# A deformable-convolution network: the first pair's sums moved to the front, its weights spread by three engines, and half of its rows kept on chip

## The chip, the cores and the metric

The kernel runs on one core of a Trainium2 chip. The metric is the device time of the whole program in microseconds (us). Five engines work side by side, each in the order of its own list of instructions: TensorE (PE: matrix products and transposes), VectorE (DVE), ScalarE (ACT), GpSimd (POOL) and SyncE (SP), which here does nothing but issue transfers. ACT and POOL issue transfers too. An engine waits at an instruction until the semaphores that it names are reached, and everything behind it in that engine's list waits with it.

## The reference, cut to what matters

The input `x` has 8 images of 64 channels and 128 x 128 pixels. Four layers follow one another, each `x = x + layer(groupnorm(x))`: a deformable convolution (layer 0), a 3x3 convolution, a two-way state-space scan, and a layer of nearest neighbours. Only layer 0 is touched, and of it only the beginning:

```
xn     = groupnorm(x)                        # 32 groups: two channels each, over all pixels
offset = conv(xn, wh: 1x15) + conv(xn, wv: 15x1) + bh + bv      # 18 maps
mask   = sigmoid(conv(xn, wm: 3x3) + bm)                         # 9 maps
y      = sum over 9 taps of wd[tap] @ (mask * bilinear sample of xn at pixel + tap + offset)
x      = x + relu(batchnorm(y))
```

The group's mean and variance need all pixels of an image before one of them can be normalized; the samples of a pixel can lie anywhere in the image.

## The kernel before, in words

Two images of 64 channels fill the 128 partitions, so the work goes by 4 pairs. For each pair layer 0 has these parts, all in `deform` (lines 177 to 446, with its helpers):

- `statistics(p)` (L262): eight loads of 16 rows (128 x 2048, 1 MB each) into two alternating buffers `xs`; VectorE takes the sums of 512 columns at a time (`bn_stats`, L269); `groupnorm` (L139) makes from them the scale `r` and the bias `nb` (L147).
- `fill(p)` (L274): the same eight pieces are loaded again (L287, tile `xt`, the same two buffers), ScalarE normalizes each in place (L288), PE transposes four rows at a time (L291, 33 steps `g`), VectorE and ScalarE copy the transposed rows out of PSUM into `q` (L293 to L295; three buffers), and SP writes `q` to two tables in DRAM (L301), in which an entry holds a pixel and the one below it with all 64 channels. With the rim of zeros around it, one entry and its neighbour give all four corners of a bilinear sample in 1 KB.
- `offsets(p, e)` (L305): for 8 rows at a time, a piece `xe` of `x` is loaded (L311) and normalized (L312), PE makes the three convolutions at once with block-diagonal weights `wt` (L323, tile `po`, one PSUM buffer), ScalarE adds the bias (`ob`, L333), PE transposes the maps (`to`, L336), and `positions` (L342) turns them into indices and weights on VectorE (L350 to L372).
- `sample(p, g, ...)` (L377): GpSimd issues 9 indirect loads for each of 8 blocks of a row group (L389, tile `g`, four buffers of 9 loads); VectorE multiplies and adds the corners (L398, L399), PE transposes (L403), ScalarE copies (L406), PE applies `wd` (L412).

Before the first `sample`, the kernel has to make: zero rims of four tables (L198 to L206, from a tile `zeros`), the loads and the spreading of the weights into `wt` (L207 to L223: from the loaded `whv` and `wmm`, 28 copies on VectorE, 28 on GpSimd, 2 sums and 18 more copies on VectorE), the bias, `statistics(0)`, `fill(0)` and `offsets(0, 0)`. Then the loop at the end of `deform` (from L427 on) runs `sample` for pair 0, with small steps of the next `offsets` and of `far` mixed in: `far` is the setup of layers 2 and 3 (`self.setup`, many small loads and small VectorE operations), then `statistics` and `fill` of the next pair. After all pairs, `rest` does the other layers.

The order written in Python isn't the order on the chip: a scheduler of the framework orders each engine's list by dependencies and by its own estimate of times, gives buffers out, and lets an instruction whose inputs are ready move up. So the setup of layers 2 and 3 begins in the very first microseconds. Two of its habits matter here. A buffer that is allocated where an earlier one was released waits for the readers of the earlier one: in the kernel before, the buffers `xs` lie over the setup tiles `zeros`, `whv` and `wmm`. And all transfers of SP and ACT share eight completion semaphores in turn, so that a transfer is not issued before the one eight places ahead of it in the common order has landed.

Of the kernel before, what the change touches and what calls it, by code (L numbers as in the profile page):

```python
# [9 lines left out]
F32 = mybir.dt.float32  # L10
# [6 lines left out]
P = 128  # L17
C = 64
H = 128
HW = H * H  # L20
CH = 512
NCH = HW // CH
ROOM = 2 * (H // 2 + 1) * H
CELL = H + 3
LINE = H + 4
PW = 2 * C
# [15 lines left out]
class Net:  # L42
# [134 lines left out]
    def deform(self):  # L177
        tc, nc, ins = self.tc, self.nc, self.ins
# [4 lines left out]
        at = {t: n for n, t in enumerate(taps)}  # L183
        with ExitStack() as ctx:
# [4 lines left out]
            wt = cp.tile([P, len(taps), 3, 2, 9], F32, name="wt")  # L189
            nc.gpsimd.memset(wt, 0.0)  # L190
            bias = cp.tile([54, 1], F32, name="bias")
# [1 line left out]


            tables = [[self.dram.tile([CELL, LINE, PW], F32, name=f"table{s}{i}") for i in range(2)] for s in range(min(2, self.npair))]
            with tc.tile_pool(name="a_setup", bufs=1) as sp:
                zeros = sp.tile([P, 2 * PW], F32, name="zeros")
                nc.gpsimd.memset(zeros, 0.0)  # L198
                for table in (t for pair in tables for t in pair):
                    flat = table.rearrange("a b q -> a (b q)")  # L200
                    n = LINE * PW // P
                    for row in (0, CELL - 1):
                        nc.scalar.dma_start(flat[row : row + 1, :].rearrange("a (p n) -> (a p) n", p=P), zeros[:, 0:n])
                    for r0, r1 in ((1, CELL - 1 - 1), (CELL - 2, CELL - 1)):
                        nc.scalar.dma_start(flat[r0:r1, 0 : 2 * PW], zeros[0 : r1 - r0, :])
                        nc.scalar.dma_start(flat[r0:r1, (LINE - 2) * PW :], zeros[0 : r1 - r0, :])  # L206
                whv = sp.tile([P, 2, 15, 2, 9], F32, name="whv")  # L207
                wmm = sp.tile([P, 9, 9], F32, name="wmm")
                for i in range(2):
                    rows = slice(i * C, (i + 1) * C)  # L210
                    nc.sync.dma_start(whv[rows, 0], ins["wh"])
                    nc.sync.dma_start(whv[rows, 1], ins["wv"])
                    nc.sync.dma_start(wmm[rows], ins["wm"])
                for i in range(2):
                    rows = slice(i * C, (i + 1) * C)
                    for d in range(-7, 8):
                        if d:
                            nc.vector.tensor_copy(wt[rows, at[0, d], 0:2, i, :], whv[rows, 0, d + 7])
                            nc.gpsimd.tensor_copy(wt[rows, at[d, 0], 0:2, i, :], whv[rows, 1, d + 7])
                    nc.vector.tensor_add(wt[rows, 0, 0:2, i, :], whv[rows, 0, 7], whv[rows, 1, 7])  # L220
                    for a in range(3):
                        for b in range(3):
                            nc.vector.tensor_copy(wt[rows, at[a - 1, b - 1], 2, i, :], wmm[rows, 3 * a + b])  # L223
                bh = sp.tile([36, 2], F32, name="bh")
                for d in range(2):
                    for i in range(2):
                        to = slice(18 * d + 9 * i, 18 * d + 9 * i + 9)
                        for n, b in enumerate(("bh", "bv")):
                            nc.sync.dma_start(bh[to, n : n + 1], ins[b][d].rearrange("(k o) -> k o", o=1))
                nc.vector.tensor_add(bias[0:36, :], bh[:, 0:1], bh[:, 1:2])  # L230
                for i in range(2):
                    nc.sync.dma_start(bias[36 + 9 * i : 45 + 9 * i, :], ins["bm"].rearrange("(k o) -> k o", o=1))
            wt = wt.rearrange("p t d i k -> p t (d i k)")
            wd = cp.tile([P, 5, C], F32, name="wd")
            nc.sync.dma_start(wd[:, 0:4, :], ins["wd"][0:512].rearrange("(j p) o -> p j o", p=P))
            nc.sync.dma_start(wd[0:C, 4, :], ins["wd"][512:576])

            xp = pool("a_x", 2)
            ep = pool("a_e", 2)
# [19 lines left out]
            norms = {}  # L259
            ready = {}  # L260

            def statistics(p):  # L262

                st = wp.tile([P, NCH, 6], F32, tag="gst", name=f"st{p}")
                for n in range(8):
                    xs = xp.tile([P, 2048], F32, tag="xs", name=f"xs{p}_{n}")
                    nc.sync.dma_start(xs, self.x[p * P : (p + 1) * P, n * 2048 : (n + 1) * 2048])
                    for m in range(4):
                        nc.vector.bn_stats(st[:, 4 * n + m, :], xs[:, m * CH : (m + 1) * CH])  # L269
                    yield  # L270
                norms[p] = self.groupnorm(wp, ps_s1, "s1", st, "gn0")
                yield

            def fill(p):  # L274

                r, nb = norms[p]
                table = tables[p % len(tables)]

                q = qp.tile([P, 2, 4, 2, C], F32, tag="q", name=f"q{p}_0")
                nc.gpsimd.memset(q[:, :, 0, 0, :], 0.0)  # L280
                for g in range(NCH + 1):
                    n = 4 if g < NCH else 1
                    if g < NCH:
                        if g % 4 == 0:
                            xs = xp.tile([P, 16, H], F32, tag="xs", name=f"xt{p}_{g}")
                            xf = xs.rearrange("p h w -> p (h w)")
                            nc.sync.dma_start(xf, self.x[p * P : (p + 1) * P, g * CH : (g + 4) * CH])  # L287
                            nc.scalar.activation(xf, xf, AF.Identity, bias=nb, scale=r)  # L288
                        tp = ps_t.tile([P, 4, 2, C], F32, tag="tp", name=f"tp{p}_{g}")
                        for m in range(4):  # L290
                            nc.tensor.transpose(tp[:, m].rearrange("p i c -> p (i c)"), xs[:, 4 * (g % 4) + m, :], self.ident)  # L291
                        nxt = qp.tile([P, 2, 4, 2, C], F32, tag="q", name=f"q{p}_{g + 1}")
                        nc.vector.tensor_copy(q[:, :, :, 1, :].rearrange("p i r c -> p r i c"), tp)  # L293
                        nc.scalar.copy(q[:, :, 1:4, 0, :].rearrange("p i r c -> p r i c"), tp[:, 0:3])
                        nc.vector.tensor_copy(nxt[:, :, 0, 0, :], tp[:, 3])  # L295
                    else:
                        nc.gpsimd.memset(q[:, :, 0, 1, :], 0.0)
                    for i in range(2):
                        rows = table[i][4 * g + 1 : 4 * g + 1 + n]
                        src = q[:, i, 0:n].rearrange("p r t c -> p r (t c)")  # L300
                        nc.sync.dma_start(rows[:, 2 : 2 + H, :].rearrange("r w e -> w r e"), src)  # L301
                    q = nxt
                    yield
# [114 lines left out]
            def run(steps):  # L418
                for _ in steps:
                    pass  # L420

            run(statistics(0))
            run(fill(0))
            run(offsets(0, 0))
            for p in range(self.npair):  # L427
                more = p + 1 < self.npair
                far = chain(statistics(p + 1), fill(p + 1)) if more else iter(())
                if p == 0:  # L430
                    far = chain(self.setup(ps_s1, "s1"), far)
                for e in range(NCH // 2):
                    if e == NCH // 2 - 1:
                        run(far)
                    nxt = (p, e + 1) if e + 1 < NCH // 2 else (p + 1, 0)
                    near = offsets(*nxt) if nxt[0] < self.npair else iter(())
                    count = [0]

                    def work(near=near, far=far, count=count):
                        count[0] += 1  # L440
                        next(near, None)
                        if count[0] % 3 == 0:
                            next(far, None)

                    idx, wts = ready.pop((p, e))
                    for half in range(2):
                        sample(p, 2 * e + half, tables[p % len(tables)], idx, wts[half], work)
                    run(near)
# [930 lines left out]
```

## Time and profile before

| what | us |
|---|---|
| median of 3 runs | 16689.37 |
| lowest and highest | 16679.99 and 16696.37 |
| the profiled execution, its own time | 16687.07 |
| its span | 16685.0 |
| PE / VectorE / ScalarE / GpSimd busy in the span | 11226.6 / 11600.4 / 2990.4 / 10394.8 |
| first and last start of a gather (L389) | 167.9 and 11883.7 |

The profile is of one execution; times in it count from the start of its span, which is 2.07 us shorter than that execution's time. A line of a timeline has start, duration, engine, source line, operation, output and input, and in brackets how long the engine had been idle and what ended that. "SPq" and "ACTq" are issues of transfers. A "window" table has the busy time of each engine in a stretch, the granted clock of PE as a share of full speed, and how busy the 16 DMA engines were.

### The profile page before, as it was taken

How to read it: one execution, taken by the hardware profiler on the slowest of the kernel's cores; microseconds unless marked ns; L12 is line 12 of the kernel's file. 1: busy time of each engine (PE TensorE's matmuls, PEld its weight loads, DVE VectorE, ACT ScalarE, POOL GpSimd, SP SyncE). 2: the span in 40 equal slices, each digit the busy share in tenths (PEclk: the TensorE clock that was granted, in tenths of full speed). 3: DMA queues.
4: the chain of work that ended last, by engine and by line, in shares of the span. 5: the costliest groups of instructions: out<-in, count | busy, mean ns of one | idle time of the engine just before them, and what ended most of it. 6: DMA issues, size and time to landing. Idle time of an engine off the chain costs nothing. (4 is left out here: it accounts for less than half of the span.)

```text
span 16685.0 us, 119663 instructions
## 1 busy us (share of the span) xinstructions
PE 11226.6 (67%) x31864; PEld 4101.4 (25%) x31864; DVE 11600.4 (70%) x27208; ACT 2990.4 (18%) x5596; POOL 10394.8 (62%) x10484
## 2 busy tenths in 40 slices
PE   6766565756576655667566566663489888988896
PEld 1211111111111111111111111111144344444443
DVE  6777777777777777777777777777557557566566
ACT  1101111111110011111000110100144243243342
POOL 4777777777777777777777777777434134043142
PEclk9987787878787787878778788776689899999897
DMA  5334444444433344443333333333322433424223
GB/s 172 120 115 128 133 130 135 136 131 134 137 120 112 114 129 130 135 131 120 112 114 113 118 115 114 118 110 108 118 67 68 148 77 104 112 78 133 85 67 103
DMA packets 900631, 1937.61 MB, mean 116 GB/s; under 512 B 199916, under 2 KB 435828, under 8 KB 876404
## 3 DMA queue, kind: packets, MB, share of 16 engines
q0 software_dynamic: 442368, 1208.55, 24.4%
q1 hardware_dynamic: 383204, 684.00, 13.4%
q10 hardware_dynamic: 74384, 37.40, 1.1%
q8 instruction: 260, 4.26, 0.1%
q14 instruction: 415, 3.40, 0.1%
HBM read 1544.92 MB, written 208.10 MB: 105 GB/s over the span
## 5 line engine op out<-in xcount | busy, mean ns | idle before, releaser
L389 POOL DMA_INDIRECT g<-table,idx x9216 | 8908.4, 967 | 2809.5 <-issue 2613.6
L398 DVE TENSOR_TENSOR g<-g,wts 128x256 f32<-128x256 f32 x9216 | 3818.1, 420 | 3101.9 <-DMA g<-table,idx 3084.0
L399 DVE TENSOR_REDUCE sm<-g 128x64 f32<-128x256 f32 x9216 | 4988.3, 580 | 0.8 <-DVE pos L353 0.2
L323 PE MATMUL po<-xe,wt 128*54 128x512 f32 (+3 forms) x8384 | 4734.9, 676 | 44.4 <-ACT ob L333 42.5
L403 PE MATMUL sp<-ident,sm 128*128 128x128 f32 x4096 | 1525.1, 377 | 4117.6 <-DVE sm L399 4100.3
L403 PEld LDWEIGHTS sp<-ident,sm 128*128 128x128 f32 x4096 | 626.2, 155 | 6897.7 <-DVE sm L399 4964.4
L406 ACT COPY s<-sp 128x512 f32<-128x512 f32 x1024 | 600.0, 586 | 8514.1 <-PE sp L403 8514.1
L323 PEld LDWEIGHTS po<-xe,wt 128*54 128x54 f32 x8384 | 929.9, 140 | 1417.2 <-issue 1069.3
L840 POOL COPY l_yb<-ln_y 128x512 f32<-128x512 f32 x128 | 79.1, 659 | 1303.9 <-PE l1v L834 1161.4
L412 PE MATMUL yp<-s,wd 128*64 128x512 f32 (+1 forms) x2560 | 808.1, 652 | 12.6 <-ACT s L406 12.6
L1206 POOL TENSOR_TENSOR u<-u,v 128x512 f32<-128x512 f32 x256 | 330.7, 1292 | 697.4 <-DVE v L1205 519.7
L563 PE MATMUL c<-room,l_w 128*64 128x508 f32 (+1 forms) x3072 | 741.3, 597 | 21.1 <-DMA room<-nx 14.9
L1298 POOL TENSOR_TENSOR ms<-ms,ln_y 128x512 f32<-128x512 f32 x256 | 278.4, 1107 | 738.8 <-DVE ln_y L119 706.7
L1188 ACT ACTIVATE fx<-room,ln_b,ln_g 128x512 f32<-128x512 f32 x512 | 639.2, 1293 | 116.2 <-DMA in<-fx 97.9
L405 PE MATMUL s<-ident,sm 128*64 128x128 f32 x1024 | 345.9, 338 | 363.1 <-DVE sm L399 336.1
L1221 DVE TENSOR_TENSOR_SCAN z<-tabs,z,u 128x256 f32<-128x256 f32 x512 | 444.9, 902 | 208.3 <-POOL u L1206 192.9
L1199 PE MATMUL pv<-in,tabs 128*128 128x512 f32 x1024 | 537.2, 649 | 46.2 <-DVE u L1205 46.2
L1268 PE MATMUL py<-x,outs 128*128 128x512 f32 x1024 | 506.0, 599 | 4.6 <-POOL x L1253 4.2
L1268 PE MATMUL py<-in,outs 128*128 128x512 f32 x1024 | 505.7, 606 | 1.6 <-ACT h L1270 1.2
L1285 PE MATMUL pc<-outs,h 128*128 128x256 f32 x2048 | 498.9, 394 | 9.9 <-DVE h L1271 8.8
L1253 POOL TENSOR_TENSOR x<-x,xt 128x512 f32<-128x512 f32 x256 | 350.6, 1370 | 126.3 <-DVE xt L1252 126.0
L1285 PEld LDWEIGHTS pc<-outs,h 128*128 128x128 f32 x2048 | 382.5, 195 | 168.7 <-issue 65.4
(406 smaller groups left out, 10008.7 us busy)
## 6 DMA issues: line engine op xcount, KB each, us to landing
g<-table,idx POOLq DMA_INDIRECT x9216, 2.7
in<-fx SPq DMA_DIRECT2D x1024, 128.0 KB
xe<-in_x_dram SPq DMA_DIRECT2D x56, 1408.0 KB
table<-q SPq DMA_DIRECT2D x256, 256.0 KB
xs<-in_x_dram SPq DMA_DIRECT2D x32, 1024.0 KB
xt<-in_x_dram SPq DMA_DIRECT2D x32, 1024.0 KB
y<-ys SPq DMA_DIRECT2D x128, 256.0 KB
room<-in_x_dram SPq DMA_DIRECT2D x64, 512.0 KB
```

The lines of the kernel that those rows point to most:

```text
L323: nc.tensor.matmul(po[:, r0:r1, c0:c1], lhsT=wt[:, t, :], rhs=xe[:, row + r0 : row + r1, c0 + dx : c1 + dx], start=n == 0, stop=n == len(u ...
L389: nc.gpsimd.indirect_dma_start(out=tq[:, k, :], out_offset=None, in_=flat[i], in_offset=bass.IndirectOffsetOnAxis(ap=idx[:, at : at + 1], ...
L398: nc.vector.tensor_mul(t[:, k], t[:, k], w)
L399: nc.vector.tensor_reduce(sm[:, k], t[:, k].rearrange("p q c -> p c q"), axis=mybir.AxisListType.X, op=ALU.add)
L403: nc.tensor.transpose(sp[:, j, :], sm[:, j * P : (j + 1) * P], self.ident)
L406: nc.scalar.copy(st[i][:, 0:4, m * P : (m + 1) * P], sp)
L412: nc.tensor.matmul(yp[i * C : (i + 1) * C, :], lhsT=wd[0:rows, j, :], rhs=st[i][0:rows, j, :], start=j == 0, stop=j == 4)
L563: nc.tensor.matmul(o, lhsT=lt, rhs=mv, start=k < 2, stop=k >= len(calls) - 2)
L1188: nc.scalar.activation(fx[:, e].rearrange("p h (o m) -> p h o m", m=self.INNER), src[:, e::2], AF.Identity, bias=w["ln1_b"], scale=w["ln1_g"])
L1199: nc.tensor.matmul(pv, lhsT=tabs[:, at : at + P], rhs=fx[:, :, h, :], start=h == 0, stop=h == 1)
L1268: nc.tensor.matmul(py, lhsT=lt, rhs=mv, start=n == 0, stop=n == len(calls) - 1)
L1285: nc.tensor.matmul(pc[:, i], lhsT=hs[:, h, i, m * P : (m + 1) * P], rhs=self.outs[:, CEN : MIX + P], start=True, stop=True)
```

## The change

The setup block before the pools is gone; what it did stands now behind `statistics(0)`. Three edits:

1. `statistics(0)` comes first, and its pieces are loaded before anything else on SP. The loads of `wh`, `wv`, `wm` and the biases are issued by ACT instead of SP. The zero rims follow behind the weights on ACT. Since the setup tiles are now allocated after the buffers `xs`, these no longer lie over them.
2. Of the copies that spread the weights, the 28 of `wh` go from VectorE to ScalarE (`nc.scalar.copy`); GpSimd keeps its 28 and VectorE its 20 others.
3. Pieces 4 to 7 of the first pair's eight are loaded into four buffers of their own (`kept`, 32 KB on each partition), which hold them from the sums to the tables; `fill(0, kept)` loads pieces 0 to 3 again and takes 4 to 7 from there. The pool closes after `fill(0)`. Other pairs pass no `kept` and run as before.

```diff
-            with tc.tile_pool(name="a_setup", bufs=1) as sp:
-                zeros = sp.tile([P, 2 * PW], F32, name="zeros")
-                nc.gpsimd.memset(zeros, 0.0)
-                ... (zero rims, loads and copies of the weights, biases: as below, loads on nc.sync)
-                            nc.vector.tensor_copy(wt[rows, at[0, d], 0:2, i, :], whv[rows, 0, d + 7])
-                            nc.gpsimd.tensor_copy(wt[rows, at[d, 0], 0:2, i, :], whv[rows, 1, d + 7])
             wd = cp.tile([P, 5, C], F32, name="wd")
-            nc.sync.dma_start(wd[:, 0:4, :], ins["wd"][0:512].rearrange("(j p) o -> p j o", p=P))
-            nc.sync.dma_start(wd[0:C, 4, :], ins["wd"][512:576])
...
-            def statistics(p):
+            def statistics(p, kept=()):
...
-                    xs = xp.tile([P, 2048], F32, tag="xs", name=f"xs{p}_{n}")
+                    xs = kept[n] if n in kept else xp.tile([P, 2048], F32, tag="xs", name=f"xs{p}_{n}")
...
-            def fill(p):
+            def fill(p, kept=()):
...
-                            xs = xp.tile([P, 16, H], F32, tag="xs", name=f"xt{p}_{g}")
-                            xf = xs.rearrange("p h w -> p (h w)")
-                            nc.sync.dma_start(xf, self.x[p * P : (p + 1) * P, g * CH : (g + 4) * CH])
+                            held = g // 4 in kept
+                            xf = kept[g // 4] if held else xp.tile([P, 2048], F32, tag="xs", name=f"xt{p}_{g}")
+                            xs = xf.rearrange("p (h w) -> p h w", w=H)
+                            if not held:
+                                nc.sync.dma_start(xf, self.x[p * P : (p + 1) * P, g * CH : (g + 4) * CH])
                             nc.scalar.activation(xf, xf, AF.Identity, bias=nb, scale=r)
...
-            run(statistics(0))
-            run(fill(0))
+            with tc.tile_pool(name="a_first", bufs=1) as fp:
+                kept = {n: fp.tile([P, 2048], F32, name=f"kept{n}") for n in range(4, 8)}
+                run(statistics(0, kept))
+                with tc.tile_pool(name="a_setup", bufs=1) as sp:
+                    ...
+                        nc.scalar.dma_start(whv[rows, 0], ins["wh"])
+                        nc.scalar.dma_start(whv[rows, 1], ins["wv"])
+                        nc.scalar.dma_start(wmm[rows], ins["wm"])
+                    ...
+                                nc.scalar.copy(wt[rows, at[0, d], 0:2, i, :], whv[rows, 0, d + 7])
+                                nc.gpsimd.tensor_copy(wt[rows, at[d, 0], 0:2, i, :], whv[rows, 1, d + 7])
+                    ... (2 sums and 18 copies on nc.vector; the biases, loaded by nc.scalar)
+                    zeros = sp.tile([P, 2 * PW], F32, name="zeros")
+                    nc.gpsimd.memset(zeros, 0.0)
+                    ... (the zero rims of the four tables, nc.scalar.dma_start)
+                nc.sync.dma_start(wd[:, 0:4, :], ins["wd"][0:512].rearrange("(j p) o -> p j o", p=P))
+                nc.sync.dma_start(wd[0:C, 4, :], ins["wd"][512:576])
+                run(fill(0, kept))
             run(offsets(0, 0))
```

More of the change, by code (lines that the diff above doesn't have):

```diff
@@ L195, in deform @@
             tables = [[self.dram.tile([CELL, LINE, PW], F32, name=f"table{s}{i}") for i in range(2)] for s in range(min(2, self.npair))]
-            with tc.tile_pool(name="a_setup", bufs=1) as sp:
-                zeros = sp.tile([P, 2 * PW], F32, name="zeros")
-                nc.gpsimd.memset(zeros, 0.0)
[L199 to L217, printed above, removed]
-                            nc.vector.tensor_copy(wt[rows, at[0, d], 0:2, i, :], whv[rows, 0, d + 7])
-                            nc.gpsimd.tensor_copy(wt[rows, at[d, 0], 0:2, i, :], whv[rows, 1, d + 7])
[L220 to L232, printed above, removed]
@@ L233, in deform @@
-            wt = wt.rearrange("p t d i k -> p t (d i k)")
             wd = cp.tile([P, 5, C], F32, name="wd")
-            nc.sync.dma_start(wd[:, 0:4, :], ins["wd"][0:512].rearrange("(j p) o -> p j o", p=P))
-            nc.sync.dma_start(wd[0:C, 4, :], ins["wd"][512:576])
             xp = pool("a_x", 2)
@@ L420, in run @@
                     pass
-            run(statistics(0))
-            run(fill(0))
+            with tc.tile_pool(name="a_first", bufs=1) as fp:
+                kept = {n: fp.tile([P, 2048], F32, name=f"kept{n}") for n in range(4, 8)}
+                run(statistics(0, kept))
+                with tc.tile_pool(name="a_setup", bufs=1) as sp:
+                    whv = sp.tile([P, 2, 15, 2, 9], F32, name="whv")
+                    wmm = sp.tile([P, 9, 9], F32, name="wmm")
+                    for i in range(2):
+                        rows = slice(i * C, (i + 1) * C)
+                        nc.scalar.dma_start(whv[rows, 0], ins["wh"])
+                        nc.scalar.dma_start(whv[rows, 1], ins["wv"])
+                        nc.scalar.dma_start(wmm[rows], ins["wm"])
+                    for i in range(2):
+                        rows = slice(i * C, (i + 1) * C)
+                        for d in range(-7, 8):
+                            if d:
+                                nc.scalar.copy(wt[rows, at[0, d], 0:2, i, :], whv[rows, 0, d + 7])
+                                nc.gpsimd.tensor_copy(wt[rows, at[d, 0], 0:2, i, :], whv[rows, 1, d + 7])
+                        nc.vector.tensor_add(wt[rows, 0, 0:2, i, :], whv[rows, 0, 7], whv[rows, 1, 7])
+                        for a in range(3):
+                            for b in range(3):
+                                nc.vector.tensor_copy(wt[rows, at[a - 1, b - 1], 2, i, :], wmm[rows, 3 * a + b])
+                    bh = sp.tile([36, 2], F32, name="bh")
+                    for d in range(2):
+                        for i in range(2):
+                            to = slice(18 * d + 9 * i, 18 * d + 9 * i + 9)
+                            for n, b in enumerate(("bh", "bv")):
+                                nc.scalar.dma_start(bh[to, n : n + 1], ins[b][d].rearrange("(k o) -> k o", o=1))
+                    nc.vector.tensor_add(bias[0:36, :], bh[:, 0:1], bh[:, 1:2])
+                    for i in range(2):
+                        nc.scalar.dma_start(bias[36 + 9 * i : 45 + 9 * i, :], ins["bm"].rearrange("(k o) -> k o", o=1))
+                    zeros = sp.tile([P, 2 * PW], F32, name="zeros")
+                    nc.gpsimd.memset(zeros, 0.0)
+                    for table in (t for pair in tables for t in pair):
+                        flat = table.rearrange("a b q -> a (b q)")
+                        n = LINE * PW // P
+                        for row in (0, CELL - 1):
+                            nc.scalar.dma_start(flat[row : row + 1, :].rearrange("a (p n) -> (a p) n", p=P), zeros[:, 0:n])
+                        for r0, r1 in ((1, CELL - 1 - 1), (CELL - 2, CELL - 1)):
+                            nc.scalar.dma_start(flat[r0:r1, 0 : 2 * PW], zeros[0 : r1 - r0, :])
+                            nc.scalar.dma_start(flat[r0:r1, (LINE - 2) * PW :], zeros[0 : r1 - r0, :])
+                wt = wt.rearrange("p t d i k -> p t (d i k)")
+                nc.sync.dma_start(wd[:, 0:4, :], ins["wd"][0:512].rearrange("(j p) o -> p j o", p=P))
+                nc.sync.dma_start(wd[0:C, 4, :], ins["wd"][512:576])
+                run(fill(0, kept))
```

## The prediction

> **What bounds the kernel now.** I read the page's list of costly groups first, then GpSimd's waits in the stage of the gathers, then the timelines of the first 170 us.
>
> ```profile
> L389 POOL DMA_INDIRECT g<-table,idx x9216 | 8908.4, 967 | 2809.5 <-issue 2613.6
> ```
>
> ```profile
> POOL g L389 <- issue: 2613.6, 8581, 0.3
> ...
> POOL g L389 <- DVE sm L399: 142.7, 470, 0.3
> ```
>
> From 167.9 to 11883.7 us GpSimd does nothing but gathers: 8908 us busy and 2810 us of gaps, of which none is over 0.3 us except one of 3.3. It waits for nobody, so the stage's length is fixed by GpSimd, and a change ahead of it is worth exactly what it moves the first gather. The change touches only what lies ahead.
>
> ```profile
> 162.40 0.20 POOL L297 MEMSET q<- 128x128 f32 x1 [149.94 <-ACT ob L333]
> ...
> 167.85 1.17 POOL L389 DMA_INDIRECT g<-table,idx  x1 [3.26 <-DVE up L368]
> ```
>
> The first gather (G) is at 167.85 and waits for the indices. Going back from there, in SP's and ScalarE's timelines:
>
> ```profile
> 20.08 2.44 SPq L827 DMA_DIRECT2D lre<-in_lam_re_dram  x4
> ...
> 28.54 0.91 SPq L267 DMA_DIRECT2D xs<-in_x_dram  x2
> ...
> 53.40 3.57 SPq L267 DMA_DIRECT2D xs<-in_x_dram  x2
> ...
> 61.54 3.64 SPq L287 DMA_DIRECT2D xt<-in_x_dram  x2
> ```
>
> ```profile
> 71.82 4.08 ACT L288 ACTIVATE xt<-xt,gn_nb,gn_y 128x2048 f32<-128x2048 f32 x2 [30.48 <-DVE gn_nb L147]
> 75.81 1.97 ACT L312 ACTIVATE xe<-xe,gn_nb,gn_y 128x1920 f32<-128x1920 f32 x1
> ```
>
> The first piece for the sums is asked for only at 28.5 us, after the weights and behind the setup of the scan. The norms are there at 71.7; call ScalarE's first normalization, 71.82, T0. From T0 to G it takes 96.0 us, and in that stretch two things are full at once (window table of 84 to 150 us: PE, PE weight loads, VectorE, ScalarE, GpSimd, clock, DMA share, GB/s):
>
> ```profile
> 84.00:150.00 66.00, 64.16 (x211) 22.52 (x209) 21.73 (x49) 24.26 (x31) 0.00 (x0) 1.00 1.01 296
> ```
>
> The DMA engines are at 1.01 and PE at 97%. PE carries the transposes and the first two offset convolutions, in one fixed order:
>
> ```profile
> 77.83 1.95 PE L323 MATMUL po<-xe,wt 128*54 128x512 f32 x2 [1.89 <-ACT xe L312]
> ...
> 145.40 4.33 PE L323 MATMUL po<-xe,wt 128*54 128x500 f32 x10
> ...
> 159.46 1.12 PE L291 MATMUL tp<-ident,xt 128*128 128x128 f32 x4 [5.34 <-DVE q L295]
> ```
>
> The convolutions begin at 77.83 (T0 + 6.0, when the normalized `xe` is there) and end at 149.7; the last transposes, late for their loads and for buffers, come at 159.5.
>
> **What the Trainium skill says.** "DMA: Bandwidth & Descriptors", section "Issuing engines are not separate DMA queues": transfers issued by different engines run on the same 16 DMA engines, and spreading them saves only time of issue. The trace agrees: the share is 1.01 although SP alone issues. So the loads moved to ACT bring no bandwidth; the gain is SP's free queue. "ScalarE: Activation LUTs", section "What ACT_TABLE_LOAD costs": an operation with immediate operands takes 186 ns + 0.833 ns per column, and neighbours overlap by about 93 ns. For 18 columns that is 201 ns, or 108 ns with overlap; the trace has 179 ns for a copy of 2 columns (L1219). "TensorE: Matmul & The Clock Gate", part 1: an idle PE falls to half clock and needs some microseconds of work to come back. The trace agrees: clock 0.50 from 154 to 166 us, when PE waited.
>
> **The change, part by part.** The order of the changed program's instructions shows where the scheduler put things; durations are those above.
>
> *Sums first.* The first piece's load is SP's first transfer, about 0.75 us instead of 28.5. A lone piece takes 5.85 us from issue to its first sum (36.62 to 42.56 and again 45.06 to 50.91); several in flight follow each other by 2.95 us, since 266 GB/s at 0.75 of the DMA engines (40 to 60 us) makes 355 GB/s, and a piece is 1.05 MB. If nothing else held them, eight would be in at 0.75 + 5.85 + 7 x 2.95 = 27 us. But the order holds them: piece 3 waits for its buffer (sums of piece 1, about 14.5), so it lands at 20.4; `kept5` right behind it at about 24; `kept6` shares its completion semaphore with `kept5` and is issued only when that has landed, 24 + 5.85 + a little for the rims' traffic = 30.5; `kept7` waits for the 12th rim transfer on ACT. ACT gets there so: weight loads and biases until 10.5 (one of these waits for piece 1), table load 1.28, 28 copies 3.0 to 5.6, so rims from 17 us; the first six rims took 3.3 us before (7.57 to 10.82), and one of the 12 waits for piece 3: about 24, landed at 26. So `kept7` is issued at 26.5 and lands behind `kept6` at about 33.5. Sums 2.5 us, and the norm 6.3 (7.0 before, from 64.8 to 71.82, with other work mixed in): T0 = 42.3. I keep 39 (copies at the low end, nothing held) to 48 (rims held longer). ACT is through with its rims at about 33 and doesn't hold T0; piece 0's second load goes out when `kept7` has landed and is in at about 40. Gain: 71.8 - 42.3 = 29.5 us.
>
> *Weights.* VectorE's 28 copies (4.0 us in 9.1 to 13.9) leave an idle engine: 0. ScalarE's 28 are inside T0 above. GpSimd's 28 (4.28 us) lie under the loads: 0; without that cover they would cost their 4.3.
>
> *Rows kept.* Four loads of 1.05 MB fewer at 2.95 us: 11.8 us less DMA. This is no gain while PE is full, for PE's work stays: both convolutions ran from 77.83 to 149.7, 71.9 us, of which 26 groups of transposes at 0.585 (15.2) and 1.6 of waits; so 55 us are convolution. What moves is its start. In ScalarE's new list the normalizations of `kept4` to `kept7` (2.05 each) and five copies of `q` (0.45) stand ahead of `xe`: 2 x 2.05 + 4 x 2.05 + 5 x 0.45 + 1.97 = 16.5, so PE's first convolution is at T0 + 16.6 instead of T0 + 6.0. From there PE has 25 groups of transposes (14.6), 55 of convolution, 2 for the cold clock and 0.6 for `ob`: 72.2, and it ends at T0 + 88.8. Behind it come `ob` 0.78, `to` 0.5, the copy 0.38 and the positions, 4.4 before (163.14 to 167.52) and about 1 more for setup operations that now lie between them: 7.1. Waits of PE for `q` buffers: 0 to 3, I take 1.5. G = T0 + 97.4, against T0 + 96.0. Before, the convolutions were done 18 us ahead of G and the last transposes came late; now it is the other way round. The tables are not late: 33 steps at 1.85 us (the spacing between loads, 106.1 to 112.1 and 139.3 to 144.1) plus two pieces make 67 us from T0 + 7.
>
> *Setup pushed back.* `kept` lies where the setup of the scan gets its buffers, so that setup now waits for the last transposes. Its VectorE work, 47.6 us busy in 20 to 80 less sums 19.7, norm about 4 and copies 2, is some 22 us, and goes mostly under the first gathers. There VectorE has 31 us free in 100 (68.86 busy in 160 to 260), and four buffers of 9 gathers at 1.25 us are 45 us of lead: 0; uncovered, up to 22. The load of `xe` for the next rows stands behind some 26 small loads on SP (0.62 each, 16 us), and ScalarE's copies L406 queue behind its normalization; both are done before the first nine gathers are summed. Kept at 0, bound 5. Two more table loads on ScalarE, 1.28 each, are under its idle time.
>
> Sum: G = 42.3 + 97.4 = 139.7, 28 us earlier. From the list on GpSimd after that nothing differs. The profiled execution (16687.07) would become 16659; it is 2.3 below the median, and on the median 16689.37 the forecast is **16661**, -0.17%.
>
> **Rivals.** (a) *The fill follows the DMA engines.* For it: share 1.01. Then 11.8 us of loads come off and G - T0 is about 84: 28 + 13 = 41 us, 16648. Against it: PE is 97% busy in the same window, and its order starts the convolutions 10 us later. 0.15.
> (b) *The head is held.* Each load waits for the one eight places before it, rims and pieces alternate, and two pairs of rims took 3.2 and 3.6 us before. If ACT's rims end at 35 instead of 24, `kept7` lands at 43 and T0 is 52: gain 18, 16671. Against it: the rims are small and their partners early. 0.18.
> (c) *The setup stalls the gathers.* VectorE takes its list in order; if an operation of the setup waits for one of the small loads on SP longer than the 45 us of lead, GpSimd stops, microsecond for microsecond. To be 33 us slower than before, one such hold must reach 45 + 28 + 33 = 106 us. For it: setup loads went out from 165 to 206 us before, 41 us in a row. Against it: none of them held a gather before. At that point 16723; 0.05.
> (d) *The pieces are loaded again all the same:* excluded, four loads `xt` are left in the list.
>
> **How the numbers follow.** Forecast 0.62, (a) 0.15, (b) 0.18, (c) 0.05. The forecast's own ends: T0 39 to 46 and PE's waits 0 to 3 make 16656 to 16667. The range reaches to (a) and (b) and takes in 5 us at either side for run-to-run spread (16680 to 16696 before): 16645 to 16678. 0.2% is 33 us, about what a measurement of this kernel can tell from no change; the forecast and (b) lie inside it. Faster: (a), and 0.06 of the forecast, 0.21; slower 0.05; same 0.74.
>
> **What would show it.** In the changed profile: first piece issued by 1 us; T0 at 39 to 46; PE's first convolution about 16 us after T0 and its last after the last transposes, not before; no half clock of PE ahead of the first gather; G at 135 to 146; GpSimd's gaps still 0.3. Wrong if T0 is over 48, if the convolutions' end isn't what the indices wait for, or if gathers wait for VectorE in the first 200 us.

## The result

The changed kernel takes 16659.57 us (median of 20 runs, 16640.04 to 16678.41), the kernel before beside it 16684.21 (20 runs, 16668.97 to 16722.15): the ratio is 0.9984, with a 95% interval of 0.9977 to 0.9990. A second series gave 16652.74 against 16686.49, ratio 0.9981 (0.9974 to 0.9988). The forecast was 16661, with most of its chance on a difference within 0.2%, and so it came. That it is met to 1.4 us is luck: the forecast gain was 28.4 us, and the medians of the two series differ by 24.6 and 33.8. The profiled span is 16651.1 us, 33.9 less than before; the change in the first gather's time, the safer measure, is 30.7.

The page's costliest group and GpSimd's waits in the changed kernel:

```profile
L353 POOL DMA_INDIRECT g<-table,idx x9216 | 8908.1, 967 | 2823.7 <-issue 2611.3
```

```profile
POOL g L353 <- issue: 2611.3, 8573, 0.3
POOL g L353 <- DVE sm L363: 146.2, 482, 0.3
```

The stage of the gathers is the same: 8908.1 us busy as before 8908.4, gaps of 0.3. It runs from 137.2 to 11852.9 (before 167.9 to 11883.7), so both its ends lie 30.7 or 30.8 us earlier, and what follows it differs by 3 us more in this execution. All of the gain is made ahead of the first gather. There, in the timelines of SP, ScalarE, PE and GpSimd (start, duration, engine, line, operation, count, idle time before and what ended it):

```profile
0.74 5.69 SPq L229 DMA_DIRECT2D xs<-in_x_dram  x2
...
16.59 13.35 SPq L229 DMA_DIRECT2D kept<-in_x_dram  x3
```

```profile
44.38 4.08 ACT L252 ACTIVATE xt<-xt,gn_nb,gn_y 128x2048 f32<-128x2048 f32 x2 [28.09 <-DVE gn_nb L147]
...
58.15 2.00 ACT L276 ACTIVATE xe<-xe,gn_nb,gn_y 128x1920 f32<-128x1920 f32 x1
```

```profile
60.30 4.28 PE L287 MATMUL po<-xe,wt 128*54 128x512 f32 x10
...
114.38 0.66 PE L255 MATMUL tp<-ident,kept 128*128 128x128 f32 x4
...
117.18 12.70 PE L287 MATMUL po<-xe,wt 128*54 128x508 f32 x30
130.66 0.45 PE L300 MATMUL to<-ident,ob 54*128 54x54 f32 x4 [0.77 <-ACT ob L297]
```

```profile
137.17 1.18 POOL L353 DMA_INDIRECT g<-table,idx  x1 [17.42 <-DVE up L332]
```

T0 came from 71.82 to 44.38. From there PE's first convolution comes after 15.9 us instead of 6.0, then PE works nearly without a pause to the end of the second convolution (129.9), and G follows 92.8 us after T0 (96.0 before). The last transposes now end well ahead of the convolutions; before, they came 10 us behind them (159.5 against 149.7). The window table for 60 to 130 us (PE, PE weight loads, VectorE, ScalarE, GpSimd, clock, DMA share, GB/s) shows PE at 99% and the DMA engines at 0.82 on the average:

```profile
60.00:130.00 70.00, 69.45 (x230) 24.96 (x228) 27.65 (x81) 20.34 (x33) 1.62 (x10) 1.00 0.82 238
```

### The profile page after: what moved, and what is told of

It reads as the page before. It is cut to its first block, busy times and chain, and to the rows that moved or that the text cites. A ratio compares the mean times of both kernels' runs of the same rounds, so it can differ in the third digit from the quotient of the medians.

```text
span 16651.1 us, 119639 instructions
## 1 busy us (share of the span) xinstructions
PE 11233.4 (67%) x31864; PEld 4112.4 (25%) x31864; DVE 11592.4 (70%) x27180; ACT 2995.4 (18%) x5626; POOL 10393.0 (62%) x10484
## 3 DMA queue, kind: packets, MB, share of 16 engines
q0 software_dynamic: 442368, 1208.55, 24.6%
## 5 line engine op out<-in xcount | busy, mean ns | idle before, releaser
L353 POOL DMA_INDIRECT g<-table,idx x9216 | 8908.1, 967 | 2823.7 <-issue 2611.3
L376 PE MATMUL yp<-s,wd 128*64 128x512 f32 (+1 forms) x2560 | 812.3, 654 | 12.6 <-ACT s L370 12.6
L569 PE MATMUL c<-room,l_w 128*64 128x508 f32 (+1 forms) x3072 | 742.8, 598 | 22.1 <-DMA room<-nx 15.9
L1259 POOL TENSOR_TENSOR x<-x,xt 128x512 f32<-128x512 f32 x256 | 350.6, 1370 | 126.0 <-DVE xt L1258 125.7
```

What stands on the lines that cost most here:

```text
L353: nc.gpsimd.indirect_dma_start(out=tq[:, k, :], out_offset=None, in_=flat[i], in_offset=bass.IndirectOffsetOnAxis(ap=idx[:, at : at + 1], ...
L376: nc.tensor.matmul(yp[i * C : (i + 1) * C, :], lhsT=wd[0:rows, j, :], rhs=st[i][0:rows, j, :], start=j == 0, stop=j == 4)
L569: nc.tensor.matmul(o, lhsT=lt, rhs=mv, start=k < 2, stop=k >= len(calls) - 2)
```

## The experiments

The theory was: the gain is G's shift and no more; it is made in the head, by an earlier T0; the stretch from T0 to G is bounded by PE's list of transposes and convolutions and by when that list's convolutions start; the bytes saved by keeping rows are worth nothing there. The rivals were (a), the bytes count, (b), the head is held by transfers that share a completion semaphore, and (c), the pushed-back setup stalls the gathers.

Eight of the experiments ran on two chips on which the whole program takes 12.6% longer (the kernel before at 18796.29 and 18783.52 us); the last section looks at that. The other four, beside a kernel before at 16686.49 us, are the changed kernel again, the room reserved with the sums first, the writes behind the first rows, and the last line of the table. The head is hardly touched by it: in the runs with the sums first these begin at 5.8 to 6.5 us instead of 5.7, and the runs there that have the changed kernel's sums have T0 at 44.5 to 45.3 instead of 44.1 to 44.4. So these eight are read by T0 and G in the traces, and their times only as ratios. Neither the kernel before nor the changed kernel was profiled there, so a difference of a microsecond between the two groups of runs says nothing.

| run | T0 | first convolution | G | T0 to G | ratio to the kernel before, 95% interval |
|---|---|---|---|---|---|
| before | 71.8 | 77.8 | 167.9 | 96.0 | 1 |
| changed | 44.4 | 60.3 | 137.2 | 92.8 | 0.9984 (0.9977 to 0.9990) |
| changed, again | 44.1 | 60.1 | 138.0 | 93.9 | 0.9981 (0.9974 to 0.9988) |
| sums first alone | 59.8 | 65.9 | 155.3 | 95.5 | 0.9992 (0.9982 to 1.0002) |
| kept rows alone | 59.0 | 74.8 | 151.8 | 92.8 | 0.9988 (0.9976 to 1.0000) |
| room reserved, all loaded twice | 55.1 | 70.7 | 148.8 | 93.6 | 0.9996 (0.9982 to 1.0011) |
| room reserved, sums first | 54.5 | 60.6 | 146.9 | 92.4 | one run, 16679.48 us |
| copies on VectorE | 44.5 | 61.8 | 139.7 | 95.2 | 0.9980 (0.9965 to 0.9994) |
| reads ahead of the first rows | 45.3 | 90.0 | 163.2 | 117.9 | 1.0009 (0.9992 to 1.0025) |
| writes behind them | 44.4 | 60.3 | 136.6 | 92.2 | one run, 16648.85 us |
| rims by GpSimd | 41.2 | 57.1 | 134.0 | 92.9 | 0.9987 (0.9977 to 0.9997) |
| first rows first | 44.9 | 47.1 | 128.9 | 84.0 | 0.9988 (0.9980 to 0.9997) |
| both, all rims after the norms | 38.7 | 40.8 | 127.4 | 88.8 | 0.9977 (0.9958 to 0.9995) |
| both, the second pair's rims late | 40.7 | 42.8 | 124.4 | 83.7 | 0.9974 (0.9963 to 0.9984) |

**The changed kernel again**, beside the last three runs:

> The changed kernel once more, beside the runs below on one chip. Theory: T0 at 44 to 46, T0 to G 92 to 94, G at 137 to 140, and some 31 us ahead of the kernel before on any chip, since GpSimd's stream of gathers only starts earlier. Rival (where the gathers wait for VectorE, as on the chip of the runs so far, part of the 31 us is given back): less than 15 us ahead.

It came out 33.8 us ahead in the medians, with G at 138.0: as the theory said. The rival speaks of the other group of runs, and there no run of the changed kernel was made; the intervals of that group are too wide to tell 31 us from 15.

**Each part alone.** Sums first without kept rows:

```diff
-                kept = {n: fp.tile([P, 2048], F32, name=f"kept{n}") for n in range(4, 8)}
+                kept = {}
```

(and without the pool around it)

> Edits 1 and 2 alone: the sums' loads go first and the weights are spread, but all eight pieces go through the two buffers and all eight are loaded again for the tables. My theory (the gain is the head, the kept rows bring nothing in the fill): ScalarE's first normalization (T0) at about 46, since two buffers make four turns of about 9 us, the stretch from T0 to the first gather (G) about 96 as before, G at 138 to 146, time about 16660. Rival (the kept rows carry a good part of the gain through the DMA engines): G at 150 or later, time 16668 or more.

And kept rows with the setup where it was (before's order, with the changed `statistics(0, kept)` and `fill(0, kept)`):

> Edit 3 alone: weights, rims and copies stand and run as before, ahead of the sums; half of the rows are kept. My theory: the stretch from T0 to G is about 93, as in the changed kernel, so PE's later start is there without any gain of the fill; what it gains is in the head, where the kept pieces have buffers of their own and can be asked for before the setup is through: T0 at about 57, G about 150, time about 16667. Rival (kept rows only matter as fewer bytes in the fill): T0 stays at 70 to 72 and T0 to G shrinks to 84, G about 155. If neither, T0 near 72 and G near 165.

Each alone gains about half: 12.5 us of G for the first, 16.1 for the second, 30.7 for both. For the second that is as expected (T0 59.0, G 151.8). For the first my expectation missed T0 by 14 us. But the rival isn't right in its reason: from T0 to G the two moved by 0.5 and 3.2 us only. What the kept rows bring to G comes through T0. (The 3.2 hides two larger changes: with kept rows PE's first convolution comes 9.8 us later after T0, and from it to G takes 13.0 us less. The part on the bytes returns to that.) Why T0 moves, VectorE's timeline of the run with the sums first alone tells in part:

```profile
28.85 2.47 DVE L231 BATCH_NORM_STATS2 st<-xs 128x6 f32<-128x512 f32 x4 [4.20 <-DMA xs<-in_x_dram]
42.49 0.06 DVE L595 MEMSET edt_e<- 128x2 f32 x1 [11.18 <-DMA table<-zeros]
...
43.73 4.84 DVE L231 BATCH_NORM_STATS2 st<-xs 128x6 f32<-128x512 f32 x8
```

Without kept rows the setup of the scan gets the place of the weights' tiles and of `zeros`. Its first operation, a fill of 2 columns, must wait until the rims are written out of that place, and VectorE, which takes its list in order, stands 11.2 us with the sums of two pieces behind it. The four kept buffers push that setup behind the fill. Two runs take this effect by itself. The first reserves the buffers and loads their pieces a second time:

```diff
-                run(statistics(0, kept))
+                run(statistics(0))
...
-                            if not held:
+                            if True:
```

> The changed kernel, but nothing is kept from the sums: all eight pieces are summed out of the two common buffers, and the four buffers kept are only reserved, and loaded (a second time) for the tables. So the four extra loads are back, and the setup of the scan still has to wait behind the reserved space. In the run with the sums first alone, T0 was 59.8, and VectorE stood 11.2 us at a small operation of that setup that waited for the rims. Theory (about half of what the kept rows bring is that they push the setup out of the head): T0 at 46 to 51. Rival (it is the buffers of their own, so that loads aren't held by sums): T0 at 57 or later. T0 to G: 92 to 95 in both, G at 139 to 145 or at 150 and more.

T0 at 55.1 lies between the two expectations: the hold is gone, but second loads of three pieces ran among the sums' own, since their buffers were free. So it was made again with the room reserved, but nothing loaded into it (one copy of a single column, once the last rows are normalized, keeps it taken):

```diff
-                kept = {n: fp.tile([P, 2048], F32, name=f"kept{n}") for n in range(4, 8)}
+                kept, room = {}, fp.tile([P, 4 * 2048], F32, name="room")
...
+                            if p == 0 and g == NCH - 4:
+                                nc.gpsimd.tensor_copy(room[:, 0:1], xf[:, 0:1])
```

> The sums-first-alone kernel (every piece through the two buffers and loaded twice), with the room of the four kept buffers reserved and unused until the last rows are normalized, so that only the place of the scan's setup differs. Theory (the setup's first operation on VectorE, which waits for the rims, holds the sums): the wait of 11.2 us is gone, T0 at 49 to 54 instead of 59.8, T0 to G about 95, G at 144 to 149. Rival (the two buffers and the completion semaphores set the sums' pace whatever VectorE does): T0 at 58 to 60.

VectorE now waits for its pieces alone:

```profile
28.72 2.47 DVE L231 BATCH_NORM_STATS2 st<-xs 128x6 f32<-128x512 f32 x4 [4.38 <-DMA xs<-in_x_dram]
38.49 2.47 DVE L231 BATCH_NORM_STATS2 st<-xs 128x6 f32<-128x512 f32 x4 [7.30 <-DMA xs<-in_x_dram]
```

T0 is 54.5, just outside the 49 to 54 expected, and 5.3 before the 59.8 of sums first alone. Of the 15.4 us by which the kept rows bring T0 forward, some 5 are thus the setup's place. (The two runs are of different groups, which differ by half a microsecond at the first sums.) The other 10 go with the way of all pieces through two buffers, but hardly as waits for sums. In the first 60 us SP waits ahead of these loads, by the profile, 14.6 us in this run for rims and 1.7 for sums, in the changed kernel 5.5 and 2.2.

With two buffers SP stands longer for the rims, which share the completion semaphores of the pieces. And its list has the loads of `wd` and of the first rows among the pieces, where the changed kernel has them behind. Which of the two makes the 10 us was not tested.

**Weights.** ScalarE's copies back on VectorE:

```diff
-                                nc.scalar.copy(wt[rows, at[0, d], 0:2, i, :], whv[rows, 0, d + 7])
+                                nc.vector.tensor_copy(wt[rows, at[0, d], 0:2, i, :], whv[rows, 0, d + 7])
```

> The changed kernel with ScalarE's 28 weight copies given back to VectorE, the rest as changed. Theory (VectorE is idle between the sums, and the rims come a little earlier on ScalarE): T0 within 42 to 46, G within 135 to 139, no difference that can be timed. Rival (the spread was needed, since the copies stand between the sums on VectorE and wait for their weights there): T0 at 48 or later.

T0 is 44.5, as with the copies on ScalarE: the spreading is worth nothing for T0. G is 0.7 us later than expected and 2.5 later than in the changed kernel. Of that, 1.4 is that PE's first convolution comes 17.3 us after T0 instead of 15.9, which stays unexplained, and 0.7 that `off`'s copy (L301) waited 2.0 us in VectorE's list behind operations of the setup, which in the changed kernel cost it 1.3.

**Do the bytes count?** First, the four saved loads put back as reads into a spare place in memory:

```diff
+                            if held:
+                                nc.sync.dma_start(spare[g // 4 - 4], self.x[p * P : (p + 1) * P, g * CH : (g + 4) * CH])
```

(the loads of the other pieces stay; `spare` is four new tiles in memory)

> The changed kernel with the four loads that it saved put back as idle traffic: while the tables are made, each kept piece is also read from memory and written to a spare place in memory that nobody reads (so the output is the same, and what it does is extra). Theory (PE bounds the stretch from T0 to G, the bytes saved are worth nothing there): T0 to G stays at 92 to 95, and the DMA share between 45 and 130 us rises by 0.1 or more. Rival (the bytes count): T0 to G grows by 10 to 12, to about 104.

Both expectations failed: the stretch grew by 25 us. The timelines of SP and PE say how:

```profile
38.52 1.87 SPq L251 DMA_DIRECT2D spare<-in_x_dram  x3
...
80.92 0.89 SPq L277 DMA_DIRECT2D xe<-in_x_dram  x1
```

```profile
89.97 3.23 PE L289 MATMUL po<-xe,wt 128*54 128x512 f32 x6
```

With these transfers in the list, the scheduler put the first rows' load (`xe`, at 37.3 in the changed kernel) behind 24 table writes. PE's first convolution came 44.7 us after T0, and from it to G took 73.2. This was no test of bytes but of order. So the same amount of traffic was placed behind the first rows:

```diff
+                            if held:
+                                nc.sync.dma_start(spare[g // 4 - 4], xf)
```

> The changed kernel with four pieces' worth of idle traffic that stands behind the loads of the first rows, not ahead: each kept piece, once it is normalized, is also written to a spare place in memory (extra work, nothing reads it). PE's convolutions then start where they did. Theory (PE bounds the stretch, bytes are worth little): PE's first convolution at T0 + 15 to 17, T0 to G at 92 to 96. Rival (bytes count one for one): T0 to G at 103 or more.

The DMA share in 60 to 130 us rises from 0.82 to 0.92, and G is no later (the window table, GpSimd's timeline, and PE's):

```profile
60.00:130.00 70.00, 69.62 (x229) 25.28 (x228) 26.18 (x68) 20.25 (x32) 1.36 (x9) 1.00 0.92 287
```

```profile
136.56 1.18 POOL L355 DMA_INDIRECT g<-table,idx  x1 [5.02 <-DVE up L334]
```

```profile
126.02 0.66 PE L257 MATMUL tp<-ident,kept 128*128 128x128 f32 x4
...
131.39 0.45 PE L302 MATMUL to<-ident,ob 54*128 54x54 f32 x4 [0.77 <-ACT ob L299]
```

But the tables are later. Their last transposes come at 126.0 us instead of 114.4 and 115.2 in the two profiles of the changed kernel. These 11 us or so are about what the prediction set for four pieces (11.8), and the DMA share is 1.06 from 74 to 89 us and 1.00 from 89 to 104: the tables follow the DMA engines, as rival (a) says. G doesn't move, because the convolutions, which start late, end last in both runs (the transpose of their maps, `to`, is at 131.4 here, at 130.7 and 131.5 there). So rival (a) fails for G in this order of PE's work. In the kernel before, where the convolutions began 6.0 us after T0, the tables were last.

**Is it PE, and its start?** The first rows' load, normalization and first taps put ahead of the tables:

```diff
-                run(fill(0, kept))
-            run(offsets(0, 0))
+                first = offsets(0, 0)
+                next(first)
+                run(fill(0, kept))
+            run(first)
```

> The changed kernel, with the first rows' load for the offsets, its normalization and its first taps put in the order ahead of the tables. My theory (PE's list of transposes and convolutions, some 70 us, bounds the stretch, and its start is late by ScalarE's list): PE's first convolution at T0 + 2 to 4 instead of T0 + 15.9, T0 to G about 80 to 84 instead of 92.8, G about 126, time about 16649. Rival (buffers and table writes set the stretch): the convolutions start early, but T0 to G stays at 90 or more and the time at 16657 to 16662.

PE's timeline:

```profile
47.07 6.43 PE L287 MATMUL po<-xe,wt 128*54 128x512 f32 x12 [5.45 <-ACT xe L276]
...
123.75 0.45 PE L300 MATMUL to<-ident,ob 54*128 54x54 f32 x4 [0.77 <-ACT ob L297]
```

As the theory said: PE starts 2.1 us after T0 and is done 78.8 after it, nearly without a pause, and the stretch is 84.0 (G, expected at about 126, came at 128.9). So the late place of the first rows made the other 8.8 us. PE starts 13.8 us earlier, but from there to G takes 81.8 us instead of 76.9, since the transposes that ran ahead of the first convolution now come within.

In this order the kept rows should count. Where no rows are kept and the convolutions begin 6.0 to 6.1 us after T0, from the first convolution to G takes 90.0 us (the kernel before), 89.4 (sums first alone) and 86.3 (room reserved, sums first), with the last transposes behind the first two convolutions. Here the last transposes come at 119.2, 4.5 us ahead of the second convolution's `to` (123.75). Moved back by the 11 us of four pieces, they would be last by some 6 or 7 us; that is an estimate from these two numbers, for no run had the first rows first and all pieces loaded twice.

**What holds the head?** The 24 rims issued by GpSimd:

```diff
-                            nc.scalar.dma_start(flat[row : row + 1, :]...
+                            nc.gpsimd.dma_start(flat[row : row + 1, :]...
```

(and the two lines below likewise)

> The changed kernel, with the 24 rims of zeros issued by GpSimd, which is idle there, instead of ScalarE, so that they leave the eight completion semaphores that the pieces use. My theory (the last pieces are held by the rims that share their semaphores): the last piece lands at about 30 instead of 35.6, T0 at 37 to 40 instead of 44.4, G at 129 to 133, time about 16653. Rival (the head is held by what the DMA engines can carry, rims and weights included): T0 at 43 to 45 and G at 136 to 138, no change.

SP's timeline and the window of 15 to 30 us, in this run and then in the changed kernel:

```profile
14.78 1.84 SPq L229 DMA_DIRECT2D kept<-in_x_dram  x3
```

```profile
15.00:30.00 15.00, 0.00 (x0) 0.00 (x0) 11.98 (x35) 2.14 (x20) 8.38 (x17) 1.00 1.01 392
```

```profile
15.00:30.00 15.00, 0.00 (x0) 0.00 (x0) 11.53 (x35) 1.28 (x13) 0.00 (x0) 1.00 0.92 321
```

The last three loads go out within 1.84 us instead of 13.35, so the semaphores did hold them. But T0 gains 3.2 us, not the 4 to 7 expected, and G comes at 134.0, not 129 to 133. Now the DMA engines are full (share 1.01 in 15 to 30 us; in the changed kernel 0.92): "DMA: Bandwidth & Descriptors", section "Issuing engines are not separate DMA queues", of the Trainium skill says that transfers of all issuers share the 16 engines, and this agrees. Rival (b) is right in kind, and worth 3.2 us in the changed kernel.

**A faster version.** Both findings, with the rims issued only when the norms are there (`zeros` multiplied by the scale `r`, which leaves zeros, so that they wait):

```diff
+                    nc.vector.tensor_scalar(zeros, zeros, norms[0][0], None, ALU.mult)
```

> The changed kernel with both findings used: the first rows' offsets are begun ahead of the tables, and the rims of zeros are issued by GpSimd and only once the norms are there, so that they don't share the DMA engines with the sums' loads. Theory: T0 at 37 to 40 (41.2 with the rims on GpSimd but at once), T0 to G 84 as with the first rows first, G at 121 to 124, some 14 us ahead of the changed kernel, so about 45 us ahead of the kernel before. Rival (the rims, now beside the table writes, hold the tables): T0 to G at 88 or more, G at 126 to 130.

T0 was right, and the rival too: at 58.9 us VectorE's next copy waited 6.8 us for a table write to give a buffer `q` free, PE stood 3.1 us behind it, and G came at 127.4. With the first pair's 12 rims at once and the second pair's issued in `fill(1)`:

```diff
+                    rims(tables[0], zeros, nc.gpsimd)
...
+                if p == 1:
+                    late = cp.tile([P, 2 * PW], F32, name="late")
+                    nc.gpsimd.memset(late, 0.0)
+                    nc.vector.tensor_scalar(late, late, r, None, ALU.mult)
+                    rims(table, late, nc.sync)
```

> The changed kernel with the first rows' offsets begun ahead of the tables, the first pair's 12 rims issued by GpSimd at once and the second pair's 12 rims only with the second pair's tables, thousands of us later. With all 24 rims at the norms, PE stood still after T0 and T0 to G was 88.8. Theory (those rims held the table writes): T0 at 38 to 41, T0 to G 83 to 85, G at 122 to 125, the earliest of all; some 14 us ahead of the changed kernel. Rival (T0 to G is lost to another cause): T0 to G at 88 again, G at 127 or later.

GpSimd's timeline:

```profile
124.39 1.08 POOL L368 DMA_INDIRECT g<-table,idx  x1 [4.56 <-DMA lim<-in_lam_im_dram]
```

Its T0 is 40.65, T0 to G 83.7, its time 16633.29 us against 16652.74 for the changed kernel and 16686.49 for the kernel before beside it. By G it is the earliest of all, 13.6 us ahead of the changed kernel beside it (138.0). In the medians it is 19 us below it (8 and 19 runs, whose ranges overlap).

## Why the prediction was right, point by point

- **GpSimd's stream fixes the rest, G is worth one for one:** shown. In the six profiles of the faster group, with G from 124.4 to 167.9, the last gather starts 11715.7 to 11721.1 us after the first. In the eight of the other group that time runs from 13762.7 to 13834.3 us, too far apart to read it there.
- **Sums first, T0 = 42.3:** measured 44.4, within 39 to 46. The order of holds was as told: `kept6` waited for `kept5`, `kept7` for a rim. VectorE's timeline has the sums of the last two pieces:

```profile
29.70 2.47 DVE L231 BATCH_NORM_STATS2 st<-kept 128x6 f32<-128x512 f32 x4 [3.40 <-DMA kept<-in_x_dram]
35.60 2.47 DVE L231 BATCH_NORM_STATS2 st<-kept 128x6 f32<-128x512 f32 x4 [3.43 <-DMA kept<-in_x_dram]
```

  `kept7` landed at 35.6 instead of 33.5. The norm took the 6.3 of the sum (38.11 to 44.38).
- **Weights, 0:** shown. ScalarE's 28 copies took 3.2 us (13.10 to 16.3), near the low end of the 3.0 to 5.6 given. That is 114 ns each; the estimate from the Trainium skill, "ScalarE: Activation LUTs", section "What ACT_TABLE_LOAD costs", was 108 with overlap, and the trace is within 6% of it.
- **Rows kept, no gain while PE is full:** right in its sum for the changed kernel, not in its reason. The window read for it (84 to 150 us) ends where PE stops being full: from 150 to 160 us PE mostly waited for the buffers `q` of the late tables, 5.34 us in one piece. Bytes do move the tables; they are worth nothing for G only because the convolutions now start late. The step was wrong in the head too: it counted only the four loads saved and PE's later start. The 15.4 us that the kept buffers bring to T0 were in my sum, but inside the step "sums first", whose chain of landings had the kept buffers in it; the 29.5 us there were told as the worth of the first edit, and alone it brings 12.0.
- **From PE's start to its end, 72.2 and 1.5 of waits:** measured 69.6 from 60.30 to 129.9. The cold clock's 2 us didn't come there (the first ten products take 4.28 us, and ten late ones of the kernel before took 4.33), nor did waits for `q`. The start at T0 + 16.6 was T0 + 15.9. What lies behind PE's end, 7.1, was 7.3.
- **G = 139.7:** measured 137.2. The late landing (+2.1) and the quicker stretch (-4.6) cancel in part, which is luck; had only one come, G would have been off by that much.
- **Setup pushed back, 0, bound 5:** no gather waited for it in either profile of the changed kernel, so (c) is out there. In the other group the profiles put waits of gathers down to operations of the setup (one of 13.3 us at 222.5 us, with the first rows first); no kernel before was profiled there to compare. And the step counted only a cost: beside the sums first alone, the setup out of the head is worth some 5 us of T0.
- **Rivals:** (a) is right for the tables and wrong for G, since the tables weren't last. (b) is true for 3.2 us of the changed kernel's head. The sign it gave did come, ACT's rims ended at 35 us; but `kept7` waits for the 12th of 24 only and landed at 35.6, not 43, and T0 never came near 52.

## What to carry to other kernels

When one engine's gapless stream sets the end, price a change ahead of it only by what it moves the first instruction of that stream, and split that into the moment the inputs are ready and the list of the engine that is full from there on. In that list ask when its first long piece of work can start: here, 8.8 us lay in where the first rows stood in the lists. Bytes saved count only where they move what ends last: 4 MB moved the tables by some 11 us and G not at all, because the convolutions ended later still. And read the window up to the very end of a stretch, where another engine can be the last. A buffer is worth more than its bytes: look what else would have been put in its place, and which engine waits there in order.

## What the runs showed of the hardware that was not expected

The same program takes 16686 us on one chip and 18784 to 18796 on two others. The difference is in the stage of the gathers. The page of the run with the first rows first, and GpSimd's waits in it:

```profile
L353 POOL DMA_INDIRECT g<-table,idx x9216 | 9731.4, 1056 | 4098.3 <-issue 2614.5
```

```profile
POOL g L353 <- DVE sm L363: 1083.0, 363, 23.1
```

Its median gather is as long as in the other group (946 ns), but the mean is 1056 instead of 967, and GpSimd is idle for 1275 us more, in waits of up to 23 us where none was over 0.3. In that stage VectorE too stands idle ahead of its reductions, which wait for nothing but its own product before them: 1854.7 us that the profile puts down to "remote", 405 times, up to 36.2 us long. No instruction of the program is named for it, and what it is stays open. PE's mean granted clock is 0.76 there and 0.82 in the other group; no run tells whether that is a cause or follows from the waits.

The granted clock in the window tables doesn't show all. From 46 to 60 us it is 1.00 in the changed kernel, yet eight transposes, with PE idle between the groups, take 1.97 us there (46.52, 51.19 and 58.26), and 1.09 where they stand between convolutions (first rows first, 53.43). Why the column doesn't show it stays open.

The completion semaphores were worth less than expected when freed (3.2 us of T0), with the DMA engines then at 1.01; and four pieces of traffic put ahead of one load cost 25 us, not through their bytes but by the place in SP's list that the load then got: the same four pieces behind it cost nothing.
